# A graph network layer on one core: the distance products of a block's third pair, the banks of conv1 and the way out of the last gate

## The chip, the cores and the metric

The kernel runs on one core of one Trainium2 chip. Inside that core, TensorE (PE) multiplies matrices into the eight banks of PSUM, ScalarE (ACT) applies functions to tiles, VectorE (DVE) does elementwise arithmetic, GpSimd (POOL) and SyncE (SP) mostly issue transfers. The metric is the device time of one execution in microseconds; before the change it is 1842.6 us, the median of three runs (1842.21 to 1846.51).

## The reference, cut to what matters

The input is `x` of 64 graphs with 256 nodes and 256 channels, and 64 adjacency matrices `adj` of 256 x 256, in fp32.

```python
h = max(layernorm(x), 0)
hc = transpose(h)                                   # channels first
c = relu(bn1(conv1d(hc, conv1_w, taps=1)))          # "conv1"
x_conv = transpose(relu(bn2(conv1d(c, conv2_w, taps=17, pad=8)) + hc))
s = h @ w_se.T + b_se                               # 3 numbers for each node
dist = sq[:, :, None] + sq[:, None, :] - 2 * s @ s.T
A = exp(-dist) * adj
x_nmp = A @ relu(h @ w_msg.T + b_msg)
gi, gh = concat(x_conv, x_nmp) @ w_ih.T + b_ih, h @ w_hh.T + b_hh
r, z = sigmoid(gi_r + gh_r), sigmoid(gi_z + gh_z)
out = x + (1 - z) * tanh(gi_n + r * gh_n) + z * h
```

## The kernel before, in words

**Tiles and stages.** Two graphs make a pair (`G` = 2), so a tile of one pair has 512 columns (`W`), one for each node, and 128 of the 256 channels on its partitions (`DC` = 2 chunks of channels). Four pairs make a block of eight graphs, and the main loop `for b in range(NB)` goes over eight blocks; its pairs are `i`, `i + 1`, `i + 2`, `i + 3`, and `nxt = i + 4` is the first pair of the next block. The convolution with 17 taps is done as a polynomial product: VectorE splits the input into transformed parts, TensorE multiplies these (`products`), VectorE and ScalarE transform back (`branch_back`, `odd_back`, `q_back`, `p_back`, `join`), and `residual` (L786) adds the block's input and lets ScalarE apply the relu. In the last block there is no next pair, and `conv1(nxt)` returns at once.

**What each function around the change does.** `affinity(i)` (L822) computes the exponentials of the distances. A pair has four products of 128 rows by 256 columns (two graphs, two chunks of rows; `q` counts them 0 to 3). Each contracts over only 9 numbers, and these stand on four different groups of 32 partitions of the tile `ZT`, one group for each `q`. ScalarE turns each product into `exp(-dist)` out of its PSUM bank (L830), and VectorE multiplies by the adjacency (L836). `conv1(i)` (L675) makes two products over all 512 columns, one for each chunk `o` of output channels, and ScalarE writes the result with bn1 and relu into `h1` (L688). `gates(i, dc, wait)` (L865) computes the recurrent unit for one chunk `dc` of channels. It makes the product `ghn`, whose reader is ScalarE at L878, then opens three accumulations `pr`, `pn` and `pz`, runs the parts of them that need only `hT` and `xnm`, calls `wait()`, and closes the three with the products of `x_conv` (`xcv`). After the first closing comes the tanh `tr` (L889), after the second L894 and the tanh `nn` (L896), after the third the tanh `tz` (L899), and then VectorE's three steps to the tile `d` (L903, L905, L907). `finish(i)` turns `d` of both chunks back with four transposes for each graph, adds the input row tile `y` (L916), stores the graph with a transfer that GpSimd issues (L917), and lets GpSimd load the next pair's `y` (L377).

**PSUM.** `acc()` hands out tiles of 512 columns from five banks, `aux()` from three; each tile takes a whole bank. A bank is handed out again in the order in which the program releases banks, that is, after the last instruction that reads the tile, in program order. The first instruction that writes the new tile then waits for that reader. `affinity` has a switch, `early`: normally its product `q` = 3 takes an `acc` bank and the other three take the three `aux` banks; with `early` all four are `aux`.

**The place of the change in a block.** In `gates(i, 0, wait)` the closure `wait` (in the main loop) lets `affinity(i + 2, True)`, then `conv1(nxt)`, stand between the opening and the closing of the three accumulations. At that time `pr`, `pn` and `pz` hold three of the five `acc` banks. The calls `affinity(i)` and `affinity(i + 1)` stand between the `products`, and `affinity(i + 3)` stands in the `wait` of `gates(i + 2, 0)` without `conv1`; all three have `early` at False.

**Order.** The schedule is manual: every engine executes its instructions in the order of the program text. `Pace` is a rough clock that decides where VectorE's queued transform steps are put between the others; it counts columns of products and of vector steps.

**The end.** After the last block's last `gates(i + 3, 1)` comes `finish(B // G - 1)`: ScalarE's `tz`, VectorE's L905 and L907 over all 512 columns, eight transposes, two additions, two stores of 256 KB by GpSimd. Then the program's closing waits begin (L1158): SyncE waits for all that is outstanding, each engine drains, and a barrier of all engines ends the span.

## Time and profile before

| What | Before |
|---|---|
| time, median of 3 | 1842.6 us |
| span of the profiled execution | 1841.8 us |
| PE busy | 1799.2 us, 98% |
| DVE busy | 1366.2 us, 74% |
| ACT busy | 728.5 us, 40% |
| POOL busy | 220.5 us, 12% |
| one block (distance of equal points in blocks 3 and 4) | 216.8 us |
| stores of `out`, issue by POOL to landing | 4.1 to 8.5 us, median 5.7 us |

How to read it: the span is the time from the first to the last instruction of one execution. Busy shares are averages over the whole span; an engine at 98% busy with products that follow each other sets the time, and what counts is where that engine stands still. The view of waits lists for each line of an engine what it waited for; the timeline lists instructions in order of time, with equal neighbours merged; the chain of waits is followed backwards from the last instruction to whatever released each step.

### The profile page before, as it was taken

The page shows a single profiled execution, that of the slowest core. Times are in us where ns is not written, and L with a number is a line of the kernel's source. Part 1 is how long each engine was busy: PE and PEld are TensorE (multiplying, and loading weights), DVE is VectorE, ACT ScalarE, POOL GpSimd, SP SyncE. Part 2 cuts the span into 40 slices and gives each one's busy share as a digit, 9 for nine tenths or more (in the row PEclk, how much of TensorE's full clock was granted, in tenths as well). Part 3 has the DMA queues.
Part 4 walks back from the last instruction along what each step waited for, and adds up shares of the span by engine and source line. Part 5 has one row for each costly group of instructions (what it writes and reads, how often), then busy time and mean ns, then how long its engine had stood idle before and what let it go on. Part 6 is the DMA issues. An engine that isn't in the chain of part 4 may idle for free.

```text
span 1841.8 us, 21877 instructions
## 1 busy us (share of the span) xinstructions
PE 1799.2 (98%) x7494; PEld 1113.6 (60%) x7494; DVE 1366.2 (74%) x2594; ACT 728.5 (40%) x1443; POOL 220.5 (12%) x359
## 2 busy tenths in 40 slices
PE   5999999999999999999999999999999999999997
PEld 3687454964569444784448645595546844487453
DVE  4879669795879849797697967888587974979422
ACT  2535532364323642255422653236432463224321
POOL 2210101100111011111012000110111110110000
PEclk9999999999999999999999999999999999999999
DMA  7777554854548444564347645384544744173011
GB/s 197 241 244 233 117 101 90 243 140 108 104 102 258 104 103 92 154 194 116 83 99 216 164 94 108 90 261 114 112 103 123 215 111 92 38 193 106 12 35 34
DMA packets 250498, 245.96 MB, mean 134 GB/s; under 512 B 143080, under 2 KB 176644, under 8 KB 250387
## 3 DMA queue, kind: packets, MB, share of 16 engines
q1 hardware_dynamic: 216362, 183.31, 36.9%
q0 software_dynamic: 31072, 58.60, 14.2%
q10 hardware_dynamic: 2953, 2.66, 0.7%
q8 instruction: 59, 0.97, 0.2%
q14 instruction: 52, 0.43, 0.1%
HBM read 156.56 MB, written 44.30 MB: 109 GB/s over the span
## 4 chain that ended last, share of the span: by engine, by line
PE 93%; issue 3%; DVE 2%; DMA 1%; POOL 1%; ACT 0%; ACTq 0%; POOLq 0%; DVEq 0%
PE acc L517 79%; PE aux L517 10%; PE aux L521 2%; PE aux L829 1%; POOL filt L717 1%; DMA taps<-in_c_wT_dram 1%; DMA points<-points 0%; DVE Yv L59 0%; DMA filt<-fo 0%; DVE T L65 0%; DVE Yv L62 0%; ACT e L830 0%; DVE msg L801 0%; DVE st L559 0%; POOL rstd L565 0%
## 5 line engine op out<-in xcount | busy, mean ns | idle before, releaser
L517 PE MATMUL acc<-xnm,w_ih 128*128 128x512 f32 x768 | 353.1, 592 | 0.0
L517 PE MATMUL acc<-hT,w_hh 128*128 128x512 f32 x768 | 350.5, 592 | 0.0
L517 PE MATMUL acc<-Yv,w_ih 128*128 128x512 f32 x768 | 342.7, 596 | 1.1 <-ACT Yv L789 1.1
L517 PEld LDWEIGHTS acc<-Yv,w_ih 128*128 128x128 f32 x768 | 145.8, 191 | 184.6 <-issue 180.9
L517 PEld LDWEIGHTS acc<-xnm,w_ih 128*128 128x128 f32 x768 | 144.7, 190 | 176.0 <-issue 174.4
L517 PEld LDWEIGHTS acc<-hT,w_hh 128*128 128x128 f32 x768 | 143.9, 190 | 164.6 <-issue 155.0
L891 DVE SCALAR_TENSOR_TENSOR gn<-tr,gn 128x512 f32<-128x512 f32 x64 | 44.1, 689 | 209.4 <-ACT tr L889 209.3
L889 ACT ACTIVATE tr<-acc,b_rz 128x512 f32<-128x512 f32 x64 | 44.0, 687 | 362.7 <-PE acc L517 362.7
L917 POOL DMA_DIRECT2D out_dram<-y x64 | 39.4, 620 | 797.6 <-DVE y L916 772.4
L517 PE MATMUL acc<-V,wb 128*128 128x128 f32 x1024 | 124.8, 275 | 0.0
L517 PE MATMUL acc<-U,wb 128*128 128x128 f32 x1024 | 124.3, 276 | 0.0
L517 PEld LDWEIGHTS acc<-U,wb 128*128 128x128 f32 x1024 | 120.4, 192 | 3.6 <-DVE T L59 2.0
L59 DVE SCALAR_TENSOR_TENSOR V<-T,V 128x256 f32<-128x256 f32 (+2 forms) x224 | 121.5, 607 | 0.3
L517 PE MATMUL acc<-hT,w_c 128*128 128x512 f32 x256 | 119.1, 609 | 1.3 <-ACT hT L633 1.3
L517 PEld LDWEIGHTS acc<-V,wb 128*128 128x128 f32 x1024 | 119.5, 192 | 0.0
L517 PE MATMUL aux<-e,msg 128*128 128x256 f32 x464 | 104.9, 379 | 0.0
L517 PEld LDWEIGHTS aux<-e,msg 128*128 128x128 f32 x464 | 87.1, 190 | 17.7 <-issue 6.9
L565 POOL TENSOR_TENSOR rstd<-rstd,neg_half 128x4 f32<-128x4 f32 x32 | 37.5, 1170 | 473.7 <-DVE shift L567 343.1
L896 ACT ACTIVATE nn<-gn,bn_columns 128x512 f32<-128x512 f32 x64 | 46.2, 722 | 115.7 <-DVE gn L894 115.7
L517 PE MATMUL aux<-w_msg,hT 128*128 128x259 f32 x384 | 89.6, 382 | 0.0
L517 PEld LDWEIGHTS acc<-hT,w_c 128*128 128x128 f32 x256 | 48.2, 194 | 60.2 <-issue 53.0
L426 ACT COPY adj<-adjh 128x1024 uint16<-128x1024 uint16 x58 | 73.9, 1344 | 23.3 <-DMA adjh<-halves_d 23.3
(160 smaller groups left out, 2715.7 us busy)
## 6 DMA issues: line engine op xcount, KB each, us to landing
wb<-filt SPq DMA_DIRECT2D x376, 256.0 KB
y<-in_x_dram POOLq DMA_DIRECT2D x64, 256.0 KB, 5.8
out_dram<-y POOLq DMA_DIRECT2D x64, 256.0 KB, 5.7
x<-in_x_dram SPq DMA_DIRECT2D x60, 256.0 KB
halves_d<-halves SPq DMA_DIRECT2D x116, 128.0 KB
adjh<-halves_d POOLq DMA_DIRECT2D x116, 128.0 KB, 6.2
hh<-halves SPq DMA_DIRECT2D x108, 128.0 KB
filt<-fo POOLq DMA_DIRECT2D x18, 252.0 KB, 5.4
```

The source lines that it names most:

```text
L59: return self.step(out, lambda: self.v.scalar_tensor_tensor(out, x, s, y, op0=ALU.mult, op1=ALU.add))
L426: nc.scalar.copy(v[:, j], u[:, j])
L517: nc.tensor.matmul(p, w, v, **kw)
L521: nc.tensor.transpose(p, v, ident)
L565: nc.gpsimd.tensor_tensor(t["rstd"], t["rstd"], neg_half, ALU.pow)
L717: eng.dma_start(out=filt[m][g * KG:g * KG + size].rearrange("k t c o -> (k t) (c o)"), in_=t[:size * kinds])
L829: nc.tensor.matmul(p[:, :N], ZT[rows_q, :P], ZT[rows_q, P:], start=True, stop=True)
L889: nc.scalar.activation(tr, pr, AF.Tanh, bias=b_rz[:, dc:dc + 1], scale=0.5)
L891: nc.vector.scalar_tensor_tensor(gn, tr, 1.0, gn, op0=ALU.add, op1=ALU.mult)
L896: nc.scalar.activation(nn, gn, AF.Tanh, bias=b_ih[:, 2 * DC + dc:2 * DC + dc + 1])
L917: nc.gpsimd.dma_start(out=rows(out, G * i + g), in_=row_tile(Y[i], g))
```

## The change

The change does three things. In `affinity` the switch `early` goes, so that product `q` = 3 of the block's third pair takes an `acc` bank too, as in the other pairs. In return `conv1` gets a parameter for where its second chunk takes its bank, and the call in `wait` gives it `aux`: in that place two `acc` and four `aux` tiles are handed out after the change as before. The third edit concerns the very last gate (pair 31, chunk 1): there `tz` and the two vector steps after it run graph by graph, over 256 columns each, and `finish` for one graph follows at once, with its store issued by SyncE in place of GpSimd. In all other gates the instructions and their order within each engine remain; the allocation of the tiles `tz` and `d` is moved up two lines of text.

```diff
-    def conv1(i):
+    def conv1(i, other=acc):
...
-            p = acc()
+            p = acc() if o == 0 else other()
...
-    def affinity(i, early=False):
+    def affinity(i):
...
-                p = acc() if q == 3 and not early else aux()
+                p = acc() if q == 3 else aux()
...
         nc.scalar.activation(nn, gn, AF.Tanh, bias=b_ih[:, 2 * DC + dc:2 * DC + dc + 1])
+        tz = late.tile([P, W], FP, name="tz")
+        d = OT[i, dc] = late.tile([P, W], FP, name="d", bufs=3)
         product(pz, xc, z, False, True)
-        tz = late.tile([P, W], FP, name="tz")
-        nc.scalar.activation(tz, pz, AF.Tanh, bias=b_rz[:, DC + dc:DC + dc + 1], scale=0.5)
-
+
+        parts = [slice(0, W)]
+        if (i, dc) == (B // G - 1, DC - 1):
+            parts = [slice(g * N, (g + 1) * N) for g in range(G)]
+        for u in parts:
+            nc.scalar.activation(tz[:, u], pz[:, u], AF.Tanh, bias=b_rz[:, DC + dc:DC + dc + 1], scale=0.5)
         pace.vector(W, pace.dve + ACT)
-        d = OT[i, dc] = late.tile([P, W], FP, name="d", bufs=3)
         nc.vector.tensor_sub(d, HT[i][:, dc, :], nn)
-        pace.vector(W, pace.pe + ACT)
-        nc.vector.scalar_tensor_tensor(d, tz, 1.0, d, op0=ALU.add, op1=ALU.mult)
-        pace.vector(W)
-        nc.vector.scalar_tensor_tensor(d, d, 0.5, nn, op0=ALU.mult, op1=ALU.add)
-
-    def finish(i):
-        for g in range(G):
+        for u in parts:
+            n = u.stop - u.start
+            pace.vector(n, pace.pe + ACT)
+            nc.vector.scalar_tensor_tensor(d[:, u], tz[:, u], 1.0, d[:, u], op0=ALU.add, op1=ALU.mult)
+            pace.vector(n)
+            nc.vector.scalar_tensor_tensor(d[:, u], d[:, u], 0.5, nn[:, u], op0=ALU.mult, op1=ALU.add)
+            if n < W:
+                finish(i, (u.start // N,), nc.sync)
+
+    def finish(i, graphs=range(G), eng=nc.gpsimd):
+        for g in graphs:
...
-            nc.gpsimd.dma_start(out=rows(out, G * i + g), in_=row_tile(Y[i], g))
+            eng.dma_start(out=rows(out, G * i + g), in_=row_tile(Y[i], g))
...
-            affinity(i + 2, True)
-            conv1(nxt)
+            affinity(i + 2)
+            conv1(nxt, aux)
...
-    finish(B // G - 1)
```

## The prediction on record

> **What bounds the kernel.** I read the page first, then TensorE's waits, then the timeline around those waits, then the end of the span.

> ```profile
> span 1841.8 us, 21877 instructions
> PE 1799.2 (98%) x7494; PEld 1113.6 (60%) x7494; DVE 1366.2 (74%) x2594; ACT 728.5 (40%) x1443; POOL 220.5 (12%) x359
> PE 93%; issue 3%; DVE 2%; DMA 1%; POOL 1%; ACT 0%; ACTq 0%; POOLq 0%; DVEq 0%
> ```

> TensorE is busy for 98% of the span and holds 93% of the chain of waits. A change pays only where it closes a gap of TensorE or shortens what follows its last product. Two of TensorE's waits (line: us in total, times, longest) touch the edit:

> ```profile
> PE aux L829 <- ACT e L830: 3.7, 8, 0.5
> PE acc L517 <- ACT Yv L789: 1.1, 1, 1.1
> ```

> The first occurs once in each of the eight blocks; the timeline of block 3 shows what it costs (start, duration, engine, line):

> ```profile
> 829.47 0.71 PE L829 MATMUL aux<-zT 9*128 9x256 f32 x6
> ...
> 830.64 0.69 PE L829 MATMUL aux<-zT 9*128 9x256 f32 x2 [0.46 <-ACT e L830]
> ...
> 831.26 3.70 PE L517 MATMUL acc<-hT,w_c 128*128 128x512 f32 x8
> ...
> 832.12 1.33 ACT L789 ACTIVATE Yv<-Yv,bn_shift 128x512 f32<-128x512 f32 x2 [0.36 <-DVE Yv L788]
> ...
> 834.80 5.31 PE L517 MATMUL acc<-Yv,w_ih 128*128 128x512 f32 x12
> ```

> A product is two instructions. Three products start together; the fourth waits for the bank that the first exponential empties and then runs alone, so conv1 starts 831.26 - 829.47 = 1.79 us after the first product. The wait alone is 0.46 us, but the reader should compare the whole with a pair whose fourth product has its own bank:

> ```profile
> 1018.00 0.49 PE L829 MATMUL aux<-zT 9*128 9x256 f32 x3
> 1018.01 0.48 PE L829 MATMUL acc<-zT 9*128 9x256 f32 x1
> ...
> 1018.64 0.49 PE L517 MATMUL acc<-U,wb 128*128 128x128 f32 x2
> ```

> All four start within 0.02 us and the next work follows after 0.64 us. All 24 such places in the trace show 0.64 us; of the eight early ones seven show 1.79 us. The last block has 2.94 us, because there no conv1 stands between and TensorE runs into the second wait:

> ```profile
> 1698.91 1.32 ACT L789 ACTIVATE Yv<-Yv,bn_shift 128x512 f32<-128x512 f32 x2
> ...
> 1699.68 2.84 PE L517 MATMUL acc<-Yv,w_ih 128*128 128x512 f32 x3 [1.08 <-ACT Yv L789]
> ```

> Last, the end of the span, and two rows of the program's closing lines (durations min/median/max in ns):

> ```profile
> 1829.25 0.69 ACT L899 ACTIVATE tz<-acc,b_rz 128x512 f32<-128x512 f32 x1 [0.33 <-PE acc L517]
> 1829.97 0.69 DVE L905 SCALAR_TENSOR_TENSOR d<-tz,d 128x512 f32<-128x512 f32 x1 [0.33 <-ACT tz L899]
> ...
> 1832.03 1.29 DVE L916 TENSOR_TENSOR y<-aux,y 128x512 f32<-128x512 f32 x2 [0.64 <-PE aux L521]
> 1833.02 1.21 POOL L917 DMA_DIRECT2D out_dram<-y  x2 [9.63 <-DVE y L916]
> ```
> ```profile
> L1158 POOLq DRAIN  x3: 51/93/7444, 1833.6 to 1841.5; - x3
> L1158 SPq DRAIN  x3: 7/7/13, 1839.3 to 1841.3; - x3
> ```

> From tz to the end are 12.57 us. The last store's semaphore is full at 1838.73 and SyncE has walked its waits by 1839.36. GpSimd's drain, queued behind its two stores, lasts until 1841.03, and the closing barrier takes 0.78 us more. So GpSimd ends the span, 1.67 us after SyncE.

> [...] The trace agrees for the `x` loads of the same pattern: for each, one early entry and then 8 of engines in the semaphore's records.

> **Part 1: the fourth product.** Removed: 1.79 - 0.64 = 1.15 us of TensorE's time in blocks 0 to 6, together 8.05 us. The bank it takes in `acc` was last read by VectorE's addition L801 of the message's fourth chunk, which ended at 819.4, ten microseconds before. Its exponential reads 405 ns rather than 384 ns and comes earlier than today. In the last block TensorE then waits for the residual's relu L789, whose input was ready at 1697.18; it is queued on ScalarE behind the four exponentials. Where four come together (1018.73) the next ScalarE instruction starts 1.07 us after the first; from 1697.47 that is 1698.54 rather than 1698.91, a gain of 0.37 us. Sum: 8.4 us.

> **Part 2: conv1's second chunk in `aux`.** The added wait is on an exponential. The oldest free `aux` bank is the first product's; its exponential ends at 830.59. TensorE wants the bank after the first chunk's four products: 830.12 + 0.53 + 3 x 0.43 = 831.93. Slack 1.3 us; with the third product's bank (exponential until 831.14) still 0.8 us. Cost nothing, hidden by conv1's first chunk. The first chunk gets `ghn`'s bank, read by L878 until 826.14. The `aux` bank is held until ScalarE's L688 at about 834.6; the next `aux` tiles come with transposes or aggregation, at about 859 in block 3, and before the third of them it has long been free. In both rings the same number is handed out, so `gates(i, 1)` meets the same banks with readers no later: its `pz` needs L894 (until 842.62) at 846.82 - 1.15 = 845.67.

> **Does the gain stay?** TensorE reaches `x_conv`'s first product at 834.80 - 1.15 = 833.65. Its first operand is ready at 832.84; the second, needed 0.86 us later, at 833.45. VectorE has no gap over 0.25 us from 828.61 to 852, but its next large idle times end on TensorE's work: 2.35 us at 852.89, 9.15 us at 875.23; ScalarE has 3.04 us at 852.17. All exceed 1.15 us, so both follow TensorE from there. Blocks 0 to 6 look alike (smallest VectorE gap there 2.03 us).

> **Part 3: the end.** Durations: 0.38 us for 256 columns out of PSUM on ScalarE (exponential row, 384 ns), 0.42 us for a vector step of 256 columns (L59, 416 ns), handovers as today. Counting from tz's start: tz's first half ends 0.38, L905 0.41 to 0.83, L907 0.86 to 1.28, transposes 1.32, addition 1.91 to 2.60, store 1 at 2.65 (today 3.77). Queued behind this addition on VectorE is the second half: L905 from 2.52, L907 to 3.39, addition 4.02 to 4.71, store 2 at 4.76 (today 4.36). The last store goes out 0.4 us *later*; what can pay is its path. No store by SyncE of this shape is in the trace. Bounds for its landing: [...] 5.1 us by the first `x` load of a pair under load (semaphore records, block 1) and by today's last store. Its first engine lands 3.6 us after issue there, the 256 KB weight loads by SyncE in 3.75 us (median); I take 3.6 us, since nothing else moves then. Landing 8.36 (today 9.48), SyncE's waits 0.63, barrier 0.78: end at 9.77 against 12.57, 2.8 us less [...]. GpSimd's drain then stands behind its load of `y`, issued until 1823.4; if it lasts 6.8 us after that as today, it is over before tz's second half. The moved allocations of `tz` and `d` cost nothing: the same writers wait for the same readers.

> **Forecast.** 1842.6 - 8.4 - 2.8 = 1831.4 us.

> **Rivals.**
> (a) The end gains nothing: a SyncE store on eight engines lands like a second `x` load, 6.4 us after issue; end at 4.76 + 6.4 + 1.41 = 12.57. Time 1834.2 us. For it: the shape; against: those loads queue behind their twin, these stores are 2.1 us apart.
> (b) The saved time comes back as a wait for the residual in every block, as in the last: 8 x 0.37 + 2.8 = 5.8 us, 1836.8 us. Against: the slack of 0.8 us.
> (c) Slower: the `acc` ring hands conv1's first chunk the fourth product's bank. conv1 then waits for the fourth exponential, which ends at 831.42: 831.47 instead of 831.26, 7 x 0.2 = 1.4 us worse, and 0.4 us better in the last block; with (a)'s end 1843.6 us. Against: `ghn`'s bank has been free longer.

> **Chances.** Main case 0.80, (a) 0.10, (b) 0.05, (c) or another new wait 0.05. The range starts at 1829.5 (the end at its best, less 0.9 us for the scatter of runs), and reaches up to 1836.0, over (a) and most of the way to (b). Faster by 0.3% means under 1837.1: main, (a), (b), 0.95; same 0.03, slower 0.02.

> **What would show it.** Right: L829 shows no wait on L830 and `aux` and `acc` products four together everywhere; 0.64 us to conv1; blocks of 215.6 us instead of 216.8; SyncE's last wait about 8.4 us after tz, GpSimd's drain no longer last. Wrong: TensorE waiting for L830 at conv1, for L789 in blocks 0 to 6, or a SyncE store that lands later than 5 us.

## The result, and the profile after

The changed kernel takes 1833.45 us on the median of six runs (1830.12 to 1835.3) against 1842.43 us before; the ratio is 0.9947 with a 95% interval of 0.9934 to 0.9961, which is 7 to 12 us less. A second comparison with other runs of both gave 1832.56 against 1842.33 us, ratio 0.9946 (0.9931 to 0.9962). The forecast was 1831.4 us, range 1829.5 to 1836.0.

The page of the profiled execution, head and chain:

```profile
span 1828.3 us, 21882 instructions
PE 1792.1 (98%) x7494; PEld 1110.5 (61%) x7494; DVE 1366.1 (75%) x2596; ACT 727.8 (40%) x1444; POOL 219.6 (12%) x357
PE 93%; issue 3%; DVE 2%; DMA 1%; POOL 1%; ACT 0%; SPq 0%; POOLq 0%; DVEq 0%; ACTq 0%
```

TensorE still bounds the kernel, with the same number of products in less time. In the view of TensorE's waits the line on L830 is gone. Two of its lines now bear on the change (us in total, times, longest):

```profile
PE aux L521 <- DVE d L913: 2.9, 2, 1.5
PE acc L517 <- ACT Yv L789: 1.9, 1, 1.9
```

The first is the end, now by graph, with two waits in place of one of 2.2 us; the second is the last block's wait for the residual, longer than before (1.1 us). The timeline of block 3 (start, duration) at the same place as in the prediction:

```profile
824.96 0.49 PE L829 MATMUL aux<-zT 9*128 9x256 f32 x3
824.98 0.48 PE L829 MATMUL acc<-zT 9*128 9x256 f32 x1
...
825.60 1.98 PE L517 MATMUL acc<-hT,w_c 128*128 128x512 f32 x4
...
827.42 1.88 PE L517 MATMUL aux<-hT,w_c 128*128 128x512 f32 x4
...
829.14 2.31 PE L517 MATMUL acc<-Yv,w_ih 128*128 128x512 f32 x5
```

The four products start together, conv1 follows 0.64 us after the first, its second chunk starts without a gap in `aux`, and the products of `x_conv` come 4.18 us after the first distance product instead of 5.33 us.

The last block, same view:

```profile
1689.46 1.35 ACT L789 ACTIVATE Yv<-Yv,bn_shift 128x512 f32<-128x512 f32 x2
...
1690.25 3.27 PE L517 MATMUL acc<-Yv,w_ih 128*128 128x512 f32 x7 [1.89 <-ACT Yv L789]
```

And the end of the span:

```profile
1818.13 0.84 ACT L905 ACTIVATE tz<-acc,b_rz 128x256 f32<-128x256 f32 x2 [0.33 <-PE acc L517]
...
1820.15 0.69 DVE L924 TENSOR_TENSOR y<-aux,y 128x512 f32<-128x512 f32 x1 [0.64 <-PE aux L521]
...
1820.87 2.74 SPq L925 DMA_DIRECT2D out_dram<-y  x2
...
1822.28 0.69 DVE L924 TENSOR_TENSOR y<-aux,y 128x512 f32<-128x512 f32 x1 [0.64 <-PE aux L521]
```

The closing lines (durations min/median/max in ns, first and last start):

```profile
L1165 POOLq DRAIN  x3: 51/93/7338, 1811.6 to 1828.1; - x3
L1165 SPq DRAIN  x3: 7/7/13, 1827.5 to 1827.8; - x3
```

A drain is one of the program's closing instructions. GpSimd's long one now starts at 1811.6 and is over 0.8 us after tz began; SyncE, waiting for the last store, ends the span.

To see where the time went I cut each trace at three instructions: the first distance product of the program, the first distance product of the last block's third pair, and the last gate's first `tz`. The kernels below for which no time of the whole is given ran once each and are read by the stages of that one execution. In us:

| Stage | before | after | after, second | banks alone (e1_ring) | end alone (e2_end) |
|---|---|---|---|---|---|
| start to first distance product | 117.75 | 116.72 | 116.82 | 117.73 | 118.38 |
| to the last block's third pair | 1578.98 | 1570.93 | 1570.94 | 1570.98 | 1579.41 |
| to the last tz | 132.52* | 130.48 | 132.17* | 132.17* | 130.82 |
| tz to the end | 12.56 | 10.22 | 10.26 | 12.56 | 10.25 |

A star marks a stage in which TensorE ran at half clock for 3.4 us: the granted clock was 0.50 from 1699.80 to 1703.21 in the kernel before and over 1690.70 to 1694.10 in the second execution of the changed kernel, and the banks alone have the same 132.17 us as the latter; the section on the hardware comes back to that. The second and the fourth row belong to the change: 8.05 us and 2.3 us. The first row is the start, which the change does not touch and which alone scatters over 3.4 us among the thirteen executions traced here (116.72 to 120.13). The third row differs by 0.35 us between the old and the new banks, with the star and without it (130.82 to 130.48, 132.52 to 132.17). In the second row the two executions with the old banks differ by 0.43 us; the end alone has one wait there, of 0.23 us on L671, that the others do not have.

### The profile page after: what moved, and what is told of

The parts are those of the page before. It is cut to its first block, busy times and chain, and to the rows that moved or that the text cites. A ratio compares the mean times of both kernels' runs of the same rounds, so it can differ in the third digit from the quotient of the medians.

```text
span 1828.3 us, 21882 instructions
## 1 busy us (share of the span) xinstructions
PE 1792.1 (98%) x7494; PEld 1110.5 (61%) x7494; DVE 1366.1 (75%) x2596; ACT 727.8 (40%) x1444; POOL 219.6 (12%) x357
## 4 chain that ended last, share of the span: by engine, by line
PE 93%; issue 3%; DVE 2%; DMA 1%; POOL 1%; ACT 0%; SPq 0%; POOLq 0%; DVEq 0%; ACTq 0%
PE acc L517 78%; PE aux L517 11%; PE aux L521 2%; PE aux L829 1%; DMA x<-in_x_dram 1%; POOL filt L717 1%; DVE Yv L59 0%; DVE T L65 0%; DVE Yv L62 0%; DMA filt<-fo 0%; DVE st L559 0%; POOL rstd L565 0%; DVE msg L801 0%; POOL bn_scale L595 0%; DVE y L924 0%
## 5 line engine op out<-in xcount | busy, mean ns | idle before, releaser
L517 PE MATMUL acc<-xnm,w_ih 128*128 128x512 f32 x768 | 353.1, 592 | 0.0
L517 PE MATMUL acc<-hT,w_hh 128*128 128x512 f32 x768 | 350.5, 592 | 0.0
L517 PE MATMUL acc<-Yv,w_ih 128*128 128x512 f32 x768 | 341.0, 593 | 1.9 <-ACT Yv L789 1.9
L517 PEld LDWEIGHTS acc<-Yv,w_ih 128*128 128x128 f32 x768 | 145.2, 190 | 184.3 <-issue 181.7
L517 PEld LDWEIGHTS acc<-xnm,w_ih 128*128 128x128 f32 x768 | 144.7, 190 | 176.0 <-issue 173.9
L517 PEld LDWEIGHTS acc<-hT,w_hh 128*128 128x128 f32 x768 | 143.9, 190 | 164.6 <-issue 154.3
L517 PE MATMUL acc<-V,wb 128*128 128x128 f32 x1024 | 124.8, 275 | 0.0
L517 PE MATMUL acc<-U,wb 128*128 128x128 f32 x1024 | 124.2, 276 | 0.0
L517 PEld LDWEIGHTS acc<-U,wb 128*128 128x128 f32 x1024 | 120.4, 192 | 3.5 <-DVE T L59 2.0
L59 DVE SCALAR_TENSOR_TENSOR V<-T,V 128x256 f32<-128x256 f32 (+2 forms) x224 | 121.5, 606 | 0.3
L517 PEld LDWEIGHTS acc<-V,wb 128*128 128x128 f32 x1024 | 119.5, 192 | 0.0
L517 PE MATMUL acc<-hT,w_c 128*128 128x512 f32 x228 | 106.1, 606 | 2.3 <-ACT hT L633 1.3
L517 PE MATMUL aux<-e,msg 128*128 128x256 f32 x464 | 104.9, 379 | 0.0
L517 PEld LDWEIGHTS aux<-e,msg 128*128 128x128 f32 x464 | 87.1, 190 | 17.7 <-issue 6.9
L517 PE MATMUL aux<-w_msg,hT 128*128 128x259 f32 x384 | 89.6, 382 | 0.0
L517 PEld LDWEIGHTS aux<-w_msg,hT 128*128 128x128 f32 x384 | 72.1, 190 | 17.5 <-issue 7.6
```

The costliest lines, as they stand in the source:

```text
L59: return self.step(out, lambda: self.v.scalar_tensor_tensor(out, x, s, y, op0=ALU.mult, op1=ALU.add))
L517: nc.tensor.matmul(p, w, v, **kw)
```

## The experiments

Two theories stood at the start. *Company*: the shared bank costs 1.15 us in each of seven blocks, since the fourth product not only waits but also loses the company of the other three; its own bank gives this back, and the end gives some 2.3 us. *End and scatter*: the bank edits matter little, and the gain is in the end and in the scatter of the runs. Beside them stood two questions: whether conv1's move to `aux` is needed, and which half of the third edit, working by graph or SyncE's stores, carries the end.

**The bank edits alone.** Taken from the diff: the hunks of `conv1`, `affinity` and `wait`; the last gate and `finish` as before.

> The two bank edits alone (fourth product in acc, conv1's second chunk in aux); the last gate and its outputs as before. Theory (the fourth product's own bank frees TensorE time): 0.64 us from the first product to conv1 in blocks 0 to 6, so 8.05 us less up to the last block, 0.35 us less at its wait for the residual, and about 12.6 us from tz to the end as before: 1842.4 - 8.4 = 1834.0 us. Rival (the bank edits change little and the 9 us come from the end and from the scatter of runs): 1840 us or more.

Measured: 1834.38 us (five runs) against 1843.16 us, ratio 0.9946 (0.9933 to 0.9958). All seven places show 0.64 us, the last block's 2.60 us, and the second stage of the table is the changed kernel's. *End and scatter* falls: this edit alone carries most of the gain.

**The end alone.** The other hunks of the diff; banks as before.

> The last gate by graph with stores by SyncE alone; banks as before. Theory: 1.79 us from the first product to conv1 in blocks 0 to 6 as before, and 10.2 us from tz to the end instead of 12.6: 1842.4 - 2.4 = 1840.0 us. Rival (the end carries most of the gain): 1836 us or less.

Measured: 1841.17 us (21 runs) against 1843.16 us (25 runs), ratio 0.9989 (0.9982 to 0.9997). The wait on L830 is back as it was before the change:

```profile
PE aux L829 <- ACT e L830: 3.7, 8, 0.5
```

The end takes 10.25 us from tz, and the median is nearer to the theory's 1840.0 us than to the rival's 1836 us. So the two parts add up: 8.8 + 2.0 us by the medians, 8.05 + 0.35 + 2.3 = 10.7 us by the stages.

**What a shared bank costs.** All four products of the first and second pair of every block share the three `aux` banks as well (the switch `early` is back in `affinity`).

```diff
-        affinity(i)
+        affinity(i, True)
...
-        affinity(i + 1)
+        affinity(i + 1, True)
```

> The changed kernel with all four products of a block's first and second pair in aux banks, as the third pair had them before. Theory (a shared bank costs 1.15 us of TensorE's time, since the fourth product also loses its company): 16 places go from 0.64 to 1.79 us, 18.4 us longer, span about 1847 us. Rival (only the visible gap of 0.46 us counts): 7.4 us longer, about 1836 us.

Measured, in the view of TensorE's waits and by the stages:

```profile
PE aux L829 <- ACT e L830: 7.4, 16, 0.5
```

The visible waits sum up to 7.4 us, but the stretch from the first distance product to the last block's third pair takes 1589.29 us instead of 1570.93 us: 18.36 us for 16 places, 1.15 us each. All 16 places show 1.79 us. The view of waits tells 40% of what the shared bank costs; the rest is the fourth product running alone. (The span, 1851.7 us, is longer than the forecast 1847 us: this execution also has the longest start, 120.13 us, 3.4 us over the changed kernel's, and 1.6 us more in the last two stages, about as much as the star is worth between the two executions of the changed kernel, 1.69 us.)

**Was the move to `aux` needed?** conv1's second chunk goes back to `acc`.

```diff
-            conv1(nxt, aux)
+            conv1(nxt)
```

> The changed kernel with conv1's second chunk back in acc, so that three acc and three aux tiles are handed out there. Theory (only the fourth product needed a bank; the ring gives conv1's second chunk the fourth product's bank, whose exponential ends half a microsecond before TensorE wants it): no wait of conv1 on L830, blocks of 215.6 us, span within 1 us of the changed kernel's apart from half-speed stretches. Rival (the move to aux is needed to pay for the bank): a wait of conv1 or of the next gate in every block, 0.3 us or more, blocks of 215.9 us or longer.

Block 3 of this kernel, timeline of TensorE:

```profile
825.80 0.48 PE L829 MATMUL acc<-zT 9*128 9x256 f32 x1
...
826.42 3.70 PE L517 MATMUL acc<-hT,w_c 128*128 128x512 f32 x8
829.96 2.31 PE L517 MATMUL acc<-Yv,w_ih 128*128 128x512 f32 x5
```

conv1 runs through its eight instructions without a gap, TensorE has no wait on L830, and the blocks last 215.6 to 215.8 us from the second on, as in the changed kernel. The move is harmless, as predicted, but not needed: with three tiles from `acc` the second chunk waits for nothing that is late.

**By graph, but with GpSimd's stores.**

```diff
-                finish(i, (u.start // N,), nc.sync)
+                finish(i, (u.start // N,))
```

> The changed kernel with the last gate by graph, but its two stores issued by GpSimd as before. Theory (what ends the span is GpSimd's drain, some 7 us behind its last store, so the gain of the end is SyncE's path): store 2 issued about 4.9 us after tz's start, drain until 12.3 us, end 13.1 us after tz, that is 0.5 us later than before the change. Rival (working by graph is what pays): end about 11.5 us after tz or earlier.

Measured: end 12.69 us after tz, against 12.56 us before the change and 10.22 us with SyncE.

```profile
L1165 POOLq DRAIN  x3: 51/93/6432, 1824.3 to 1831.2; - x3
L1165 SPq DRAIN  x3: 7/7/13, 1829.0 to 1831.0; - x3
```

GpSimd's drain is the last again. It was over sooner than I expected (11.9 us after tz, not 12.3): here and before the change it ends 2.3 us after the last store has landed (9.60 and 9.48 us), but 5.8 and 6.8 us after that store's issue was over. So its length follows the landing and not the issue.

**The whole tile, but with SyncE's stores.** The last gate and `finish` over 512 columns as before, with `eng=nc.sync`.

> The changed kernel with the last gate over all 512 columns as before, and its two stores issued by SyncE. Theory (the issuing engine is what pays; working by graph delays the second store by 0.8 us and only parts the two): stores issued at about 3.5 and 4.15 us after tz, the second queues behind the first on eight engines and lands 5.5 us after issue, end about 10.8 us after tz against 10.2 in the changed kernel. Rival (the split is worthless): end at 9.5 us or earlier.

```profile
1818.88 0.69 ACT L905 ACTIVATE tz<-acc,b_rz 128x512 f32<-128x512 f32 x1 [0.33 <-PE acc L517]
...
1822.37 1.35 SPq L923 DMA_DIRECT2D out_dram<-y  x2
```

Measured: end 10.03 us after tz, 0.2 us *sooner* than by graph. A store counts as landed at the last entry that the trace has for its semaphore, the counter that SyncE's closing waits read. The stores go out at 3.50 and 4.24 us and land at 7.53 and 8.87 us; by graph they go out at 2.75 and 4.87 us and land at 6.79 and 9.06 us. So the issuing engine carries the whole gain of the end, 2.5 us, and working by graph gives 0.2 us back, because the second graph's steps stand behind the first graph's addition. I had expected the opposite sign, since I had put the second store's queueing at 1.3 us; it was 0.6 us (landing 4.63 us after issue instead of 4.04).

**VectorE's order.** Both graphs' steps before the first addition.

```diff
-            if n < W:
-                finish(i, (u.start // N,), nc.sync)
+        if len(parts) > 1:
+            finish(i, eng=nc.sync)
```

> The changed kernel with VectorE's two steps of the second graph ahead of the first graph's addition; stores by SyncE as in the change. Theory (queued behind the first addition, the second graph waits on VectorE for 0.7 us and on TensorE for 0.6 us more): store 1 at 2.9 us and store 2 at 3.6 us after tz instead of 2.75 and 4.87; they share eight engines, so the second lands some 5.3 us after issue and the end is at about 10.0 us, 0.2 us better. Rival (the second store's issue sets the end): end 1.3 us earlier, 8.9 us after tz.

Measured: stores at 2.81 and 3.56 us, the second lands at 8.19 us, end 9.35 us after tz. That lies between the two expectations: the second store goes out 1.3 us earlier than in the changed kernel, takes 4.63 us to land instead of 4.19, as with the whole tile, and so lands 0.9 us earlier. With the order right, working by graph is worth 0.7 us against the whole tile.

**Sixteen engines.** The last pair's `d` is written with its columns permuted, so that partition p holds nodes 2p and 2p + 1 and a graph is stored as 128 rows; the last `y` is loaded alike.

```diff
+    def natural(t, g):
+        return t[g].rearrange("(p c) d -> p (c d)", c=MC)
...
+        last = i + 1 == B // G
+        t = gn if last else d
...
+                for k in range(u.start, u.stop, P):
+                    o = d[:, k:k + P].rearrange("p (b h) -> p h b", b=NW)
+                    a, c = (v[:, k:k + P].rearrange("p (h b) -> p h b", b=NW) for v in (t, nn))
+                    nc.vector.scalar_tensor_tensor(o, a, 0.5, c, op0=ALU.mult, op1=ALU.add)
...
-            eng.dma_start(out=rows(out, G * i + g), in_=row_tile(Y[i], g))
+            order = natural if i + 1 == B // G else rows
+            eng.dma_start(out=order(out, G * i + g), in_=row_tile(Y[i], g))
```

> The changed kernel, but the last pair's rows leave in their own order: VectorE writes d with its columns permuted (two instructions of 128 columns for one of 256), y is loaded in that order, and the store's slowest dimension is 128 on both sides in place of 8. Theory (eight engines make the landing 4.2 us): 16 engines, landing about 3 us after issue; store 2 issued 0.3 us later; end about 9.3 us after tz. Rival (the landing is latency, not transfer): landing still about 4.2 us, end 10.4 us.

Measured: the semaphore of each store has 16 engine entries instead of one early entry and 8, and the last comes 2.0 us after issue in place of 4.0 and 4.2 us. Store 2 goes out at 4.88 us, not 0.3 us later. The end is 8.05 us after tz. The landing fell by more than the halved transfer that I had expected: by the trace's records of packets, the first store's 128 packets of 2 KB run for 0.8 us instead of 2.4 us, and start 0.8 us after the issue instead of 1.3 us. The edit changes the order of a graph's rows in HBM together with the number of engines; what each of the two gives is not shown.

**The changed kernel again,** beside the two kernels that follow.

> The changed kernel once more, beside kernels that build on it. Theory (three pieces, which the stages of the trace show: 8.05 us at the fourth products, 0.35 us at the last block's wait, 2.3 us at the end): 10.7 us less than before on the median of many runs. Rival (the 9.0 us of the first comparison is the true size and a piece is lost somewhere): 9 us again.

Measured: 1832.56 against 1842.33 us, 9.8 us less, between the two expectations; the interval of the ratio, 0.9931 to 0.9962, is 7 to 13 us less and does not tell them apart.

**The residual first in the last block.**

```diff
             pace.flush(scaled)
+            if b + 1 == NB:
+                pace.flush(joined[0])
             affinity(i + 2)
```

> The changed kernel; in the last block alone the residual's steps are put ahead of the third pair's affinity, so that ScalarE runs the relu L789 before the four exponentials. Theory (TensorE's 1.9 us wait there is ScalarE's order, and its length also lets TensorE drop to half clock for 3.4 us in some executions): wait 0.6 us, 1.3 us less, and no half-speed stretch in the last block in any execution, which saves another 1.7 us in those that had one; about 2 us less than the changed kernel on the median. Rival (the residual itself comes too late): wait stays above 1.5 us.

Measured: 1830.13 us (six runs), 2.4 us less than the changed kernel on the medians; the two sets of six runs overlap, so the size is uncertain. ScalarE runs the relu before the exponentials, and TensorE's wait shrinks from 1.89 to 0.60 us:

```profile
1689.59 1.33 ACT L789 ACTIVATE Yv<-Yv,bn_shift 128x512 f32<-128x512 f32 x2 [3.54 <-DVE Yv L788]
...
1690.36 2.84 PE L517 MATMUL acc<-Yv,w_ih 128*128 128x512 f32 x6 [0.60 <-ACT Yv L789]
```

In this traced execution there is no half-speed stretch there: six of the instructions take 2.84 us, where three took as long at the granted clock of 0.50 before the change; the other runs were not traced.

**All together.** The changed kernel with the last three edits that helped: residual first, VectorE's order, 16 engines.

> The changed kernel with three additions: the residual first in the last block, VectorE's steps of both graphs ahead of the additions, and the last pair's rows stored in their own order on 16 engines. Theory (each removes its own piece): 1.3 us at the last block's wait, and the end at about 6.8 us after tz (store 2 issued at 3.6, landed 2.0 us later, closing 1.2 us) against 10.2: 4.7 us less than the changed kernel, some 5.5 us on the median with the half-speed stretch gone. Rival (GpSimd's drain or another closing wait takes over): end at 8 us or later.

Measured: 1826.18 us (four runs, 1824.39 to 1826.51) against 1842.33 us, ratio 0.9908 (0.9894 to 0.9923); on the medians 6.4 us faster than the changed kernel and 16 us faster than the kernel before. The last stage is 6.97 us long, so no other closing wait took over, and the stores take 2.0 and 2.1 us to land:

```profile
1819.84 1.28 DVE L936 TENSOR_TENSOR y<-aux,y 128x512 f32<-128x512 f32 x2
1820.55 0.93 SPq L938 DMA_DIRECT2D out_dram<-y  x2
```

## Why the prediction was right, point by point

**The fourth product: right.** Predicted 1.79 to 0.64 us in seven blocks, 8.05 us; measured 8.05 us (1578.98 to 1570.93). The step that made it right was to compare the whole stretch with that of a pair whose product has its own bank, not to take the wait of 0.46 us from the view of waits; the run with 16 more shared banks shows the same 1.15 us each.

**The last block: right in size.** Predicted 0.37 us, measured 0.35 us (2.94 to 2.60 us, and 0.35 us in the third stage). But I had the slower part of this place before my eyes and did not read it: the prediction's own line shows three instructions of 512 columns in 2.84 us, where elsewhere twelve take 5.31 us. TensorE ran at half clock there, from 0.12 us after the line's start on (granted clock 0.50 from 1699.80 to 1703.21).

**The second chunk in `aux`: right.** No wait, and the gates after it meet no new one. The run with the chunk in `acc` shows more than I had said: the move was not needed.

**Does the gain stay: right.** The first product of `x_conv` came 4.18 us after the first distance product, 5.33 - 1.15; no wait for L789 in blocks 0 to 6, and blocks of 215.63 us where 215.6 us was forecast. Rivals (b) and (c) did not happen.

**The end: right in mechanism, two terms off.** Predicted 9.77 us after tz, measured 10.22 us. Landing was 3.6 us in the sum and 4.2 us in the trace, below the bound of 5.1 us; the best case for the end, from which the range starts at 1829.5 us, was my estimate, which no trace of before showed: the fastest landing of a store there was GpSimd's, 4.1 us. tz over half the columns took 0.47 us instead of 0.38 us, so store 2 went out at 4.87 instead of 4.76 us. SyncE's remaining waits took 0.40 instead of 0.63 us, since four of its nine waits were walked while the store was still on its way; before, the first of the nine was the wait for the last store. Rival (a), 6.4 us, did not happen: the first store landed 6.79 us after tz, when the second's packets of data had run for 0.5 us of their 2.4 us (6.29 to 8.72 us after tz). What I left unsaid is that working by graph pays nothing in the order written. That GpSimd's drain came out right was in part luck: I let it last 6.8 us after the issue, and it lasted 6.6 us, but it follows the landing; in the run with all edits together, where the same load landed 3.2 us after the start of its issue instead of 5.0 us, it was over 4.8 us after the issue.

**The sum.** Predicted 11.2 us, with the end corrected 10.7 us; the comparisons gave 9.0 and 9.8 us, each with an interval 5 to 6 us wide. The time alone would not have told the main case from rival (a): 1833.45 us is nearer to its 1834.2 us than to 1831.4 us. The store's landing tells them apart. The traces place no further loss, and what is left lies within the scatter of the start (3.4 us) and of the half-speed stretch (1.69 us), which the runs cannot resolve further.

## What to carry to other kernels

Here a wait for a PSUM bank of 0.46 us in the view of waits cost 1.15 us, because the products would otherwise have run side by side: compare the time from the group's first instruction to the next work with a place where the group is whole. At the end of a kernel, look at which engine's drain ends last (2.5 us here) and at how many engines carry the last store (2.2 us, together with the order of the rows), before splitting the arithmetic (0.7 us at best). And a row in which few instructions take long deserves the division: three in 2.84 us instead of six was here the clock, at 0.50, and not a wait.

## What the runs showed of the hardware that was not expected

**Half clock after a short lull.** The view of windows (stretch; length; busy us with instructions of PE, PEld, DVE, ACT, POOL; then PEclk, the granted share of TensorE's clock, DMA share and GB/s) for the same place, just after the last block's wait, first in one execution of the changed kernel, then in another:

```profile
1690.20:1693.60 3.40, 3.35 (x8) 1.62 (x9) 3.37 (x7) 1.30 (x2) 0.00 (x0) 1.00 0.00 0
```
```profile
1690.70:1694.10 3.40, 3.40 (x5) 1.35 (x4) 3.37 (x7) 0.45 (x2) 0.00 (x0) 0.50 0.00 0
```

TensorE ran 8 instructions in one and 5 in the other, and the stage to the last tz took 130.48 and 132.17 us. The waits just before were alike, 1.89 and 1.88 us, so the length of the wait alone does not decide.

TensorE was not empty in all of the lull: the distance products fill 0.71 us of it, with the old banks 1.40 us, on 9 rows. No run moved the lull against the grid on purpose, and these two executions set no limit; what decides the clock is not shown.

**GpSimd's drain.** At the end it lasted until 2.3 us after GpSimd's own last store had landed, where that store was the last work: 11.78 after 9.48 us in the kernel before, 11.90 after 9.60 us by graph with GpSimd's stores. Where GpSimd's last transfer is a load of `y`, the drain ended 2.2 us after that load's landing, in the changed kernel (landing 5.0 us after the start of the issue) and with all edits together (3.2 us). The same store from SyncE let the span end 1.2 us after its landing, in the changed kernel.

**Engines of a store.** For 256 KB from 128 partitions to HBM, issued by SyncE with nothing but the other store of the pair moving, a store with 8 engine entries took 4.0 and 4.2 us from issue to landing in the changed kernel, and 4.6 us when it went out 0.7 us behind its twin (the whole tile, VectorE's order); with 16, and the rows in their own order, it took 2.0 to 2.1 us. The issue itself took 0.61 to 0.65 us with the slowest dimension of 8 and 0.34 us with 128. GpSimd's stores in the old row order show 16 entries as well and took 4.1 us or more, so the entries of a semaphore alone do not tell how soon a store lands.
